# Thirty-three partly filled columns of a three-layer graph network, packed at lane offsets that are summed on the chip

## The chip, the cores and the metric

The kernel runs on one core of one Trainium2 chip. The metric is the device time of one execution in microseconds (us). Engines are named as the profile names them: PE (TensorE), DVE (VectorE), ACT (ScalarE), POOL (GpSimd) and SP (SyncE). SP computes nothing here; it issues plain DMAs. POOL issues the indirect DMAs (gathers and scatters).

## The reference

A graph of 6,250 nodes with 256 features and 100,000 edges (`src`, `dst`, sorted by `dst`) goes through two attention layers of one kind, a residual and a layer norm, and one attention layer of another kind, again with residual and layer norm.

```python
def _gatv2_layer(x, src, dst, n, Wl, Wr, att, b):          # H, C = 4, 64
    xl = (x @ Wl).reshape(n, H, C)
    xr = (x @ Wr).reshape(n, H, C)
    e = leaky_relu(xl[src] + xr[dst], 0.2)
    logits = einsum('ehc,hc->eh', e, att)
    ex = exp(logits - segment_max(logits, dst)[dst])
    alpha = ex / (segment_sum(ex, dst)[dst] + 1e-16)
    return segment_sum(xl[src] * alpha[:, :, None], dst).reshape(n, H * C) + b

# layers 1 and 2: every node is also its own neighbour; elu between them
x = layernorm(x + gatv2(elu(gatv2(x))))
# layer 3: 8 heads of 32; scores s1[src] + s2[dst], softmax per dst, weighted sum of Wh[src]
x = layernorm(x + gat(x))
```

The costly part is `xl[src]`: 100,000 rows of about 1 KB, fetched in each of three layers.

## The kernel before

**Plan.** `make_plan` sorts the nodes by how many edges they have, the most first, and cuts them into 49 blocks of 128 (a node per partition). For each node it makes a list of its sources, padded with the number of an empty row (NP, whose scores come out as minus infinity). Because nodes are sorted, a block needs few columns: `columns` computes, from the sizes of the problem alone (a Poisson distribution and 3.5 standard deviations), `cols[b]`, the columns of block b: 27 for block 0 (longer lists of that block are kept apart, the "few"), 25, 24, 23, ... down to 9, 803 in all. Block b, column j, is one gather: POOL fetches 128 rows, one per partition, by 128 indices (`gather_rows`, L1438).

**Packs before.** The last column of a block is often filled in its first partitions only. `columns` chooses ten such columns (blocks 3, 13, 17, 36; 26, 40, 47, 48; 31, 43) whose worst-case sizes, rounded up to eight, add up to at most 128, and joins them in three packs. SP copies the indices of a pack's columns to one column of `pick` (`pick_rows`, L1405), POOL gathers that column once (`gather_pack`, L1410), SP copies the rows from there to the place in each block's tile (`lay_rows`, L1418) and fills the other partitions of that column with the empty row (`lack_rows`, L1426). Places are known when the program is built.

**A layer.** `layer2` (layers 1 and 2) and the last part of `tile_by_degree` (layer 3) loop over the blocks. `gather(b)` puts block b's rows into two to four tiles `g` out of nine (`rowp`, bufs=9); a tile comes free when the block that held it has been summed. In layers 1 and 2 DVE computes the scores of a block (`attend`: L1797 or L1777, L1800, L1801), ACT the exponentials, DVE and ACT multiply rows by weights (L1633, L1629), PE adds them up (L1640), and PE makes the next layer's table rows, which SP stores (L1917, L1960). In layer 3 DVE does all of that but the exponentials. `fetch(b + 2)` is issued while block b is computed, so gathers run about two blocks ahead, as far as tiles allow.

**Order.** The order on each engine's queue is the order of the program's text (`manual_schedule`); each queue is worked in order and waits on semaphores. In layer 1 a block's node row (its source list and its features) is itself gathered by POOL, one gather a block (`start1`, L1887), called by `begins(b)`: three at the start, then `begins(b + 2)` in `fetch(b)`, and those that a pack's list needs. Between layers, the 37 first gathers of blocks 0 to 2 of the next layer (`begin`, lists `soon`) are taken from the part of the table that is complete early; the others wait until the whole table is written. `spots` are the sources' places in the sorted order, read in layer 1 out of the gathered rows' last element and used as lists in layers 2 and 3.

`counts` (L1270) holds each node's number of edges, and `fits` and `done` are flags: if the lists don't fit the planned shape, or the early part was too short, a general path (`tile_general_path`) does the work instead. `spare` (L1251 to 1257) is seven gathers of list pieces that nothing reads.

The lines that the steps of the prediction touch stand in the functions below.

Of the kernel before, what the change touches and what calls it, by code (L numbers as in the profile page):

```python
# [26 lines left out]
F32 = mybir.dt.float32  # L27
# [9 lines left out]
P = 128  # L37
# [10 lines left out]
def columns(E, N, NB):  # L48
# [30 lines left out]
    part = {}  # L79
    for b in range(len(EARLY), NB):  # L80
        c = cols[b] - 1
        n = max(8, -(-int(math.ceil(over[c] + 3.5 * sd[c] - P * b)) // 8) * 8)
        if n < P:
            part[b] = n
    packs, taken = [], set()
    for b in sorted(part):
        if b in taken or part[b] > P * 3 // 4:
            continue
        pack, at = [], 0
        for k in range(b, NB):  # L90
            if k in part and k not in taken and at + part[k] <= P:
                pack.append((k, at, part[k]))
                at += part[k]
        if len(pack) > 1:
            packs.append(pack)
            taken.update(k for k, _, _ in pack)
    return cols, low, high, held, packs
# [569 lines left out]
def kernel(  # L667
# [22 lines left out]
    cols, low, high, held, packs = columns(E, N, NB)  # L690
# [7 lines left out]
    node_i = plan.tile([P, NB], I32, name="node_i")  # L698
    fits = plan.tile([P, 1], I32, name="fits")
# [11 lines left out]
    with tc.manual_schedule():  # L711
        make_plan(
            tc, x, src, dst, ((wl1, wr1, att1), (wl2, wr2, att2)), (b1, b2), w3, a3,
            cols, low, high, held, packs, node_i, fits, ident, eps, nobody, att, wc, wh, fixed, xl1_d,
            near_d,
        )
        nc.vector.memset(done, 0)
# [4 lines left out]
    with tc.If(ok != 0):  # L722
        with tc.manual_schedule():
            tile_by_degree(
                tc, x, att1, b1, b2, w3, a3, out, [held] + cols[1:], packs, node_i, near_d, ident, eps, nobody,
                xl1_d, att, wc, wh, fixed, done,
            )
# [8 lines left out]
def make_plan(  # L736
    ctx, tc, x, src, dst, layers, biases, w3, a3, cols, low, high, held, packs, node_i, fits, ident, eps,
    nobody, att, wc, wh, fixed, xl1_d, near_d,
# [36 lines left out]
    SPARE = 7  # L775
# [218 lines left out]
    for pack in packs:  # L994
        for b, _, n in pack:
            nc.gpsimd.tensor_scalar(
                most[:, b : b + 1], part_of, float(n), float(cols[b] - 1), op0=OP.is_lt, op1=OP.add
            )
# [252 lines left out]
    spare = one.tile([P, SPARE, LONG], I32, name="spare")  # L1251
    left(1, nc.gpsimd)
    for k in range(SPARE):
        nc.gpsimd.indirect_dma_start(
            out=spare[:, k, :], out_offset=None, in_=listed,
            in_offset=bass.IndirectOffsetOnAxis(ap=begin_i[:, k : k + 1], axis=1),
        )
# [12 lines left out]
    counts = one.tile([P, NB], F32, name="counts")  # L1270
# [26 lines left out]
def tile_by_degree(  # L1297
    ctx, tc, x, att1, b1, b2, w3, a3, out, cols, packs, node_i, near_d, ident, eps, nobody,
    xl1_d, att, wc, wh, fixed, done,
# [52 lines left out]
    late = consts.tile([P, len(EARLY)], F32, name="late")  # L1352
# [41 lines left out]
    packed = {b: (q, r, n) for q, pack in enumerate(packs) for b, r, n in pack}  # L1394
    opens = {pack[0][0]: q for q, pack in enumerate(packs)}
    shuts = {pack[-1][0]: q for q, pack in enumerate(packs)}
    picks = [consts.tile([P, len(packs)], I32, name=f"pick{k}") for k in range(2)]
    for pick in picks:
        nc.gpsimd.memset(pick, NP)
    held_rows = {}  # L1400

    def pick_rows(q, pick, of):

        for b, r, n in packs[q]:
            nc.sync.dma_start(pick[r : r + n, q : q + 1], of[:n, b, cols[b] - 1 : cols[b]])  # L1405
# [710 lines left out]
```

## Time and profile before

| what | value |
|---|---|
| median of 3 runs | 3244.62 us (3239.51 to 3245.31) |
| profiled execution | 3236.04 us, span 3234.2 us |
| granted clock of PE, mean | 0.711 |
| DVE busy | 2714.0 us (84%) |
| POOL busy | 2414.4 us (75%) |
| PE busy | 1399.5 us (43%) |
| ACT busy | 1281.5 us (40%) |
| HBM | 354.60 MB read, 40.42 MB written |

How to read it: "busy" counts an engine's instructions; between two gathers POOL needs time that counts as idle with the releaser "issue". A line such as `L1438 POOL DMA_INDIRECT g<-xl_d,near_r x1549 | 1465.6, 946 | 472.6 <-issue 417.6` says: source line, engine, operation, what is written from what, how many; busy time, mean ns of one; idle time just before them and what ended it. The 40 digits are busy tenths of 40 equal slices of the span, 81 us each. Layer 1 begins with the first gather of rows at 102.9 us, layer 2's early gathers at 1158, layer 3's at 2155.

### The profile page before, as it was taken

The numbers are of one execution on the slowest core, as the hardware profiler recorded it, in microseconds if no ns is written. First come the engines' busy times: TensorE is split into PE (matmuls) and PEld (weight loads), VectorE is DVE, ScalarE is ACT, GpSimd is POOL, SyncE is SP. The second block draws the span as 40 slices with busy tenths as digits, with TensorE's granted clock in tenths as the row PEclk, the third lists the DMA queues.
The fourth block names the chain that finished last, engine by engine and source line by source line (L and its number), as shares of the span: only waits on it lengthen the run. The fifth ranks groups of instructions, "written<-read, shape, count | busy, mean of one in ns | idle before, by whom it ended". The sixth has DMA issues, their size and how long they took to land.

```text
span 3234.2 us, 25459 instructions
## 1 busy us (share of the span) xinstructions
PE 1399.5 (43%) x5423; PEld 1123.4 (35%) x5424; DVE 2714.0 (84%) x2609; ACT 1281.5 (40%) x5161; POOL 2414.4 (75%) x2587
## 2 busy tenths in 40 slices
PE   8356657666676854666556566760000000000000
PEld 6245545555565643545444455550000000000000
DVE  8599999898899979999989999984966766766777
ACT  4234444444445535777667777770000000000000
POOL 5677777777777777777777777777777777777776
PEclk9678888778888886787788778885555555555555
DMA  9444444444444454444444444444333333333333
GB/s 262 123 113 125 119 120 122 118 122 124 123 123 126 126 146 116 122 123 129 128 123 127 133 129 134 135 129 113 108 107 109 110 108 107 109 109 110 109 110 93
DMA packets 176463, 397.64 MB, mean 123 GB/s; under 512 B 50923, under 2 KB 93955, under 8 KB 176283
## 3 DMA queue, kind: packets, MB, share of 16 engines
q0 software_dynamic: 120608, 336.86, 38.7%
q1 hardware_dynamic: 53992, 57.08, 5.8%
q10 hardware_dynamic: 1700, 1.97, 0.2%
q8 instruction: 48, 0.79, 0.1%
q14 instruction: 115, 0.94, 0.1%
HBM read 354.60 MB, written 40.42 MB: 122 GB/s over the span
## 4 chain that ended last, share of the span: by engine, by line
POOL 25%; DVE 18%; issue 14%; DMA 5%; PE 3%; ACT 0%; DVEq 0%; POOLq 0%; ACTq 0%
POOL g L1438 24%; DVE z L1800 4%; DVE lg L1801 4%; DMA g<-xl_d,near_r 3%; DVE z L1797 3%; PE acc L1640 3%; DVE z L1777 2%; DVE g L1633 2%; DMA g<-whs_d,near_r 1%; DVE weighted L1662 1%; POOL out L2040 1%; DMA out<-y,node_i 1%; DVE stats L1684 0%; DVE acc_v L1674 0%; DVE at L1600 0%
## 5 line engine op out<-in xcount | busy, mean ns | idle before, releaser
L1438 POOL DMA_INDIRECT g<-xl_d,near_r x1549 | 1465.6, 946 | 472.6 <-issue 417.6
L1640 PE MATMUL acc<-g,ident 128*128 128x256 f32 x3408 | 966.5, 452 | 631.3 <-DVE g L1633 318.4
L1640 PEld LDWEIGHTS acc<-g,ident 128*128 128x128 f32 x3408 | 778.4, 232 | 820.4 <-DVE g L1633 336.3
L1438 POOL DMA_INDIRECT g<-whs_d,near_r x756 | 719.5, 952 | 230.3 <-issue 220.5
L1629 ACT ACTIVATE g<-g,by 128x64 f32<-128x64 f32 x3080 | 744.9, 336 | 28.4 <-DVE by L1596 28.4
L1801 DVE TENSOR_REDUCE lg<-z 128x28 f32<-128x1820 f32 (+4 forms) x234 | 497.3, 2125 | 8.1
L1800 DVE TENSOR_TENSOR z<-z,at 128x1820 f32<-128x1820 f32 (+4 forms) x234 | 496.6, 2122 | 4.7
L1797 DVE TENSOR_TENSOR z<-g,pr 128x1820 f32<-128x1820 f32 (+3 forms) x138 | 299.6, 2171 | 42.9 <-DMA g<-xl_d,near_r 33.7
L1604 ACT ACTIVATE wt<-lg 128x128 f32<-128x128 f32 (+17 forms) x49 | 14.0, 285 | 801.5 <-DVE lg L1603 801.5
L1674 DVE TENSOR_REDUCE acc_v<-weighted 128x256 f32<-128x3584 f32 (+10 forms) x47 | 319.0, 6787 | 1.6
L1633 DVE TENSOR_TENSOR g<-g,at 128x256 f32<-128x256 f32 (+8 forms) x185 | 273.5, 1496 | 3.3
L1587 ACT ACTIVATE at<-lg,top 128x19 f32<-128x19 f32 (+14 forms) x392 | 115.3, 294 | 378.2 <-DVE top L1579 359.5
L1777 DVE TENSOR_TENSOR z<-g,pr 128x2080 f32<-128x2080 f32 (+4 forms) x96 | 197.8, 2061 | 72.3 <-DMA g<-xl_d,near_r 33.3
L2010 DVE TENSOR_TENSOR lg<-g,s_r 128x56 f32<-128x56 f32 (+4 forms) x111 | 22.9, 214 | 255.5 <-DMA g<-whs_d,near_r 234.6
L1662 DVE TENSOR_TENSOR weighted<-g,wt 128x1792 f32<-128x1792 f32 (+4 forms) x111 | 227.0, 2056 | 0.3
L1563 ACT COPY xT<-pt 128x256 f32<-128x256 f32 x147 | 50.2, 374 | 403.4 <-PE pt L1558 403.4
L1568 PE MATMUL pm<-wcat,xT 128*128 128x260 f32 x392 | 94.2, 383 | 1.4 <-ACT xT L1563 1.4
L1568 PEld LDWEIGHTS pm<-wcat,xT 128*128 128x128 f32 x392 | 74.2, 190 | 13.3 <-ACT xT L1563 2.1
L1587 ACT ACTIVATION_READ_ACCUMULATOR at<-lg,top 128x1 f32 x392 | 73.2, 187 | 0.0
L1568 PE MATMUL pm<-wh_cat,xT 128*128 128x272 f32 x196 | 58.6, 422 | 22.6 <-ACT xT L1563 22.6
L2040 POOL DMA_INDIRECT out<-y,node_i x49 | 49.8, 1015 | 22.8 <-issue 14.1
L1688 ACT ACTIVATE sd<-mv,eps 128x1 f32<-128x1 f32 x98 | 29.0, 296 | 91.5 <-DVE mv L1686 91.3
(267 smaller groups left out, 1591.5 us busy)
## 6 DMA issues: line engine op xcount, KB each, us to landing
g<-xl_d,near_r POOLq DMA_INDIRECT x1549, 2.8
g<-whs_d,near_r POOLq DMA_INDIRECT x756, 2.8
whs_d<-row SPq DMA_DIRECT2D x49, 132.0 KB
xl_d<-row SPq DMA_DIRECT2D x49, 130.0 KB
xr_d<-row SPq DMA_DIRECT2D x49, 130.0 KB
two<-xl_d SPq DMA_DIRECT2D x49, 130.0 KB
two<-xr_d SPq DMA_DIRECT2D x49, 130.0 KB
near_d<-x_all SPq DMA_DIRECT2D x7, 896.0 KB
```

The costliest lines, as they stand in the source:

```text
L1438: nc.gpsimd.indirect_dma_start(out=g[:, j + own - s0, :width], out_offset=None, in_=table, in_offset=source(of, b, j),)
L1568: nc.tensor.matmul(pm, xT[:, c, :], w[:, c, :], start=c == 0, stop=c == 1)
L1587: nc.scalar.activation(wt[:, :, h], lg[:, :S, h], AF.Exp, bias=top[:, h : h + 1], accum_out=den[:, h : h + 1],)
L1629: nc.scalar.mul(g4[:, t, h, :], g4[:, t, h, :], by[:, s0 + t - a0, h : h + 1])
L1633: nc.vector.tensor_mul(g4[:, :m], g4[:, :m], wt[:, s0 : s0 + m, :].unsqueeze(3).to_broadcast([P, m, H, F // H]),)
L1640: nc.tensor.matmul(acc, ident, g4[:, t], start=False, stop=s0 + t == S - 1 and not more)
L1662: nc.vector.tensor_mul(prod[:, s0 - base : s1 - base, :].rearrange("p t (h d) -> p t h d", h=H), g[:, :n, :F].rearrange("p t (h d) -> p t ...
L1674: nc.vector.reduce_sum(part, prod[:, : s1 - base, :].rearrange("p s f -> p f s"), axis=AX.X)
L1777: nc.vector.tensor_max(z, rows[0][:, :n, :W2], xr[:, None, :].to_broadcast([P, n, W2]))
L1797: nc.vector.tensor_max(z, g[:, :n, :W2], xr[:, None, :].to_broadcast([P, n, W2]))
L1800: nc.vector.tensor_mul(z, z, at[:, None, :].to_broadcast([P, n, W2]))
L1801: nc.vector.reduce_sum(lg[:, s0:s1, :], z.rearrange("p t (h d) -> p t h d", h=H2), axis=AX.X)
```

## The change

The packs are made denser, and their places are no longer fixed when the program is built. `lanes_of` takes every column whose expected fill is under three quarters (0.75 x 128), the last ones of 28 blocks: 33 "items" (block, column), with a worst-case size `top` each and 781 - 11 = 770 columns left for gathers of their own (`base[b]`). `find_lanes` counts on the chip how many nodes really use each item's column (a comparison of `counts`, a sum over partitions on PE, a running sum on DVE): item i's rows begin at lane `at[i]`, the sum of those before it. Bounds `lo[i]` and `hi[i]` are known from the statistics; a value outside them sets the flag for the general path.

SP loads a lane into a register and writes the item's list, `top[i]` entries long, to that place in DRAM (`pick_lanes`); the next item's list overwrites the unused end. 14 columns of 128 entries are read back as `picks`, each one is one gather (`gather_packs`), the gathered rows are stored in DRAM (`keep_packs`, which in layer 1 also reads the places of the rows for the later layers), and each item's rows are read from its lane into its block's tile (`lay_rows`). The surplus rows of an item belong to others, so `shut_lanes` adds minus infinity to the scores of partitions that don't use the column. A pack is gathered a block before the first item that can reach it (`upon`); its list must be full by then, so `gather` in layer 1 calls `begins` for all blocks whose lists can fall into it. In layer 1 the packs' tiles are those of `two`, in layers 2 and 3 three of their own. The seven `spare` gathers and the per-partition limits `most` of packed columns are gone.

```diff
-    part = {}
...
-    return cols, low, high, held, packs
+    return cols, low, high, held, lanes_of(N, NB, mean, pmf, over, sd, cols, low, high)
...
-    for pack in packs:
-        for b, _, n in pack:
-            nc.gpsimd.tensor_scalar(
-                most[:, b : b + 1], part_of, float(n), float(cols[b] - 1), op0=OP.is_lt, op1=OP.add
-            )
...
-    for k in range(SPARE):
-        nc.gpsimd.indirect_dma_start(
-            out=spare[:, k, :], out_offset=None, in_=listed,
-            in_offset=bass.IndirectOffsetOnAxis(ap=begin_i[:, k : k + 1], axis=1),
-        )
...
+    upon = [max(1, b - 1) for b in need]
+    pick_d = dram.tile([K * P + P, 1], I32, name="pick_d")
+    wide = [W2 + 1, W2, A1]
+    pack_d = [dram.tile([K * P + P, w], F32, name=f"pack{k}_d") for k, w in enumerate(wide)]
+    nc.sync.dma_start(pick_d.rearrange("(k p) c -> p (k c)", p=P), nowhere)
...
+    def find_lanes(zp, ps):
+        for k, values in enumerate((lo, hi, [0] + top)):
...
+                    nc.vector.memset(bound[:, k, i:j], float(values[i]))
...
+        for b, own in items_of.items():
+            nc.vector.tensor_scalar(
+                has[:, own[0] : own[-1] + 1], numbers[:, base[b] : cols[b]], counts[:, b : b + 1],
+                None, op0=OP.is_lt,
+            )
+        nc.tensor.matmul(pn, ones, has, start=True, stop=True)
+        nc.vector.tensor_scalar(shut, has, -1.0, BIG, op0=OP.add, op1=OP.mult)
+        nc.vector.tensor_tensor_scan(at, ones[:, : len(items) + 1], n, 0.0, op0=OP.mult, op1=OP.add)
+        nc.vector.tensor_max(held_at, at, bound[:, 0])
+        nc.vector.tensor_tensor(held_at, held_at, bound[:, 1], op=OP.min)
+        nc.vector.tensor_copy(lane_i, held_at[:1, : len(items)])
...
+    def lane(i):
+        _, (v,) = nc.values_load_multi_w_load_instructions(
+            lane_i[:, i : i + 1], engines=[mybir.EngineType.SP], min_val=lo[i], max_val=hi[i],
+            skip_runtime_bounds_check_because="the lane was brought within these bounds",
+        )
+        nc.sync.nop()
+        return bass.ds(v, top[i])
+    def pick_lanes(lists):
+        while written[0] < len(items) and items[written[0]][0] < lists:
+            i = written[0]
+            b, c = items[i]
+            nc.sync.dma_start(pick_d[lane(i), :], sources[: top[i], b, c : c + 1])
+            for q in range(K):
+                if filled_by[q] == i:
+                    nc.sync.dma_start(picks[0][:, q : q + 1], pick_d[q * P : (q + 1) * P, :])
+            written[0] += 1
...
+    def gather_packs(b, pool, pick, table, width):
+        for q in packs_at.get(b, ()):
+            held_rows[q] = pool(q)
+            nc.gpsimd.indirect_dma_start(
+                out=held_rows[q][:, :width], out_offset=None, in_=table,
+                in_offset=bass.IndirectOffsetOnAxis(ap=pick[:, q : q + 1], axis=0),
+            )
+    def keep_packs(b, k):
+        for q in packs_at.get(b, ()):
+            nc.sync.dma_start(pack_d[k][q * P : (q + 1) * P, :], held_rows[q][:, : wide[k]])
+            if k == 0:
+                nc.sync.dma_start(picked[:, q : q + 1], pack_d[0][q * P : (q + 1) * P, W2 : W2 + 1])
+    def lay_rows(b, rows, cut, own, k):
+        for i in items_of.get(b, ()):
...
+            nc.sync.dma_start(g[: top[i], j - s0, : wide[k]], pack_d[k][lane(i), :])
+    def lack_rows(b, rows, cut, own, table, width):
...
+                nc.sync.dma_start(
+                    g[top[i] :, j - s0, :width],
+                    bass.AP(tensor=table.tensor, offset=table.offset + NP * width,
+                            ap=[[0, P - top[i]], [1, width]]),
+                )
+    def shut_lanes(b, lg, own, H):
+        if b in items_of:
+            s = lg[:, base[b] + own : cols[b] + own, :]
+            nc.vector.tensor_add(s, s, shut[:, i0 : i0 + n].unsqueeze(2).to_broadcast([P, n, H]))
...
             def gather(b):
-                if b in opens:
-                    gather_pack(b, packp, "pack", picks[i], table, width)
-                gather_rows(b, rows, cut, 1, table, of, width, first, cols[b])
...
+                if i == 0 and b:
+                    lists = max([b + 2] + [items[filled_by[q]][0] for q in range(K) if upon[q] <= b]) + 1
+                    for k in range(min(NB, lists)):
+                        begins(k)
+                    pick_lanes(lists)
+                gather_rows(b, rows, cut, 1, table, of, width, first, base[b])
+                gather_packs(b, pack_tile, picks[i], table, width)
+                lack_rows(b, rows, cut, 1, table, width)
+                if b == 1:
+                    waiting.append(lambda: (keep_packs(b, i), lay_rows(b, rows, cut, 1, i)))
+                else:
+                    lay_rows(b, rows, cut, 1, i)
+                    waiting.append(lambda: keep_packs(b, i))
...
+                shut_lanes(b, lg, 1, H2)
...
             if i == 0:
                 find_few(work, pst)
+                find_lanes(zp, pst)
+                pick_lanes(3)
             gather(0)
...
+    nc.scalar.copy(picks[1], picked)
...
         def gather(b):
...
+            while waiting:
+                waiting.pop(0)()
+            gather_rows(b, rows, cut, 0, wh_d[:, :], spots, A1, first, base[b])
+            gather_packs(b, pack_tile, picks[1], wh_d[:, :], A1)
+            lack_rows(b, rows, cut, 0, wh_d[:, :], A1)
...
```

(`shut_lanes` is called in both `attend` functions, before the softmax; the last `gather` is that of layer 3.) Packs are gathered at blocks 1 (three), 3, 5, 7, 8, 15, 19, 20, 25, 34, 44 and 46. The lists that they need end with the columns of blocks 8, 16 and 20 for the three of block 1, then 25, 30, 35, 39, 42, 44, 46, 47 and 48.

## The prediction

> **What bounds the kernel now.** I read the page first: shares by engine, the 40 slices, the costliest groups.
>
> ```profile
> PE 1399.5 (43%) x5423; PEld 1123.4 (35%) x5424; DVE 2714.0 (84%) x2609; ACT 1281.5 (40%) x5161; POOL 2414.4 (75%) x2587
> ...
> DVE  8599999898899979999989999984966766766777
> ...
> POOL 5677777777777777777777777777777777777776
> ...
> L1438 POOL DMA_INDIRECT g<-xl_d,near_r x1549 | 1465.6, 946 | 472.6 <-issue 417.6
> ...
> L1438 POOL DMA_INDIRECT g<-whs_d,near_r x756 | 719.5, 952 | 230.3 <-issue 220.5
> ```
>
> DVE has the larger share, but POOL never varies. A gather is 946 ns busy and then 0.30 us in which POOL waits for nothing ("issue"), so one gather costs 1.25 us, and 75% busy is POOL full. Then the waits, POOL's and DVE's:
>
> ```profile
> POOL g L1438 <- issue: 658.0, 2160, 0.3
> ...
> DVE lg L2010 <- DMA g<-whs_d,near_r: 234.6, 40, 9.0
> ...
> DVE z L1797 <- DMA g<-xl_d,near_r: 33.7, 27, 3.4
> DVE z L1777 <- DMA g<-xl_d,near_r: 33.3, 19, 6.0
> ...
> POOL g L1438 <- PE acc L1640: 27.1, 86, 1.1
> ```
>
> From 98 us on POOL practically waits for nobody, and DVE waits for gathers: much in the third layer, little in the first two. Busy time by layer (about 102 to 1158, to 2155, to the end):
>
> ```profile
> 102.00:1158.00 1056.00, 685.36 (x2689) 559.06 (x2690) 960.95 (x859) 457.70 (x1877) 798.76 (x845) 0.81 0.45 121
> 1158.00:2155.00 997.00, 612.41 (x2232) 482.99 (x2231) 922.97 (x781) 699.21 (x2879) 753.76 (x797) 0.80 0.47 129
> 2155.00:3234.00 1079.00, 23.66 (x88) 16.96 (x86) 752.14 (x814) 83.92 (x263) 808.66 (x850) 0.51 0.39 108
> ```
>
> (Columns: PE, PEld, DVE, ACT, POOL, clock, DMA share, GB/s.) DVE is busy 91% and 93% of layers 1 and 2 and 70% of layer 3. So a gather less is worth 1.25 us in layer 3, and in layers 1 and 2 only where DVE still waits. Last, the boundary of layers 1 and 2: the last store of SP into the table (it landed 2.47 us after its issue), and POOL's first gather that needs the whole table.
>
> ```profile
> 1194.19 2.47 DMA xl_d<-row
> ```
>
> ```profile
> 1203.34 0.95 POOL L1438 DMA_INDIRECT g<-xl_d,soon  x1 [0.30 <-issue]
> 1204.59 0.95 POOL L1438 DMA_INDIRECT g<-xl_d,near_r  x1 [0.30 <-issue]
> ```
>
> The table is whole at 1196.7; POOL comes to it 7.9 us later, after its 37 early gathers. At the next boundary the last row goes out at 2185.84 (landed about 2188.3) and POOL comes at 2201.65.
>
> **The change, part by part.** *Gathers.* Row gathers fall from 1549 + 756 to 1503 + 733 (69 less), pack gathers rise from 9 to 42: 36 less, 12 a layer, 15.0 us of POOL a layer. The seven spare gathers (74.6 to 84.4 us) go too; I cost that at nothing, because POOL's next work waits 3.15 us for DVE's list of moves after them. The ten TENSOR_SCALARs at 14.5 us stand before a 16.5 us wait: nothing.
>
> *Node rows moved forward (layer 1).* A pack gather needs its list full, so `begins` now loads the node rows (L1887, 1.25 us each) of far later blocks first: 18 of them right before block 1's gathers instead of 4; by block 8 there are 40 in all instead of 14, by block 25 there are 48 instead of 32. None is added, but DVE starves early. Counting POOL instructions to the end of block 25: 531 before, 544 after (16 more node rows, 13 less rows, 10 more packs), so POOL is there 16.3 us later, at 783.8 for 767.5, and with DVE's 9.8 us behind it block 25's scores are done at 793.5 instead of 777.3. From block 26 to 48 DVE took 401.2 us, 382.3 busy. With POOL ahead the 18.9 us between go: wherever DVE lags 11 us or more in this trace (blocks 5 to 7, 42 to 46) its idle time is 0.0 to 0.6 us a block. Added: 14 of the new `shut_lanes` additions there, 0.20 us each by the nearest row (L1491, 128x44), 2.8. So DVE ends layer 1 at +16.2 - 18.9 + 2.8 = +0.1; I take +2 for waits on ACT that stay. Ends: 0, and +20 if no idle time is regained. Layer 1 keeps nothing of its 15 us.
>
> *The list chain on SP (new wait).* Each of the 33 columns is a register load, a nop and a list write to DRAM, and the writes overlap, so each waits for the one before; 14 of them and three reads stand before POOL's three pack gathers of block 1. Nearest rows: SP's TENSOR_LOAD took 0.76 us (L721), a list copy 0.62 us to issue (L1405), a store 2.47 us to land, the slowest landing of a write to DRAM 7.5 (near_d<-moved). A link is then 2.5 us at least, 9.0 at most (7.5 + 0.76 + 0.17 + 0.62 in a row); I take 2.6, since the load runs in the shadow of the write and xl_d<-row is the nearest in size. Node row 3 lands near 142, ten links and a read follow: 142 + 11 x 2.6 = 171. POOL's packs come at 160.5 + 23 x 1.25 = 189.3. Hidden by 18 us; it costs from 4.3 us a link on, 11 us of stall for each us more, 52 at most; an added wait can't gain, so the other end is 0. Queued behind the waiting pack gather are all later gathers. `find_lanes` before it holds DVE about 13 us (85 memsets of 0.06, 28 compares and a dozen others of 0.15 to 0.2) while it would start block 0, which is then still being gathered (POOL till 136.8): nothing. It also gives the register loads.
>
> *Lanes back to tiles.* Packs are stored (42 stores), read back (99 lanes instead of 30 copies), 54 fills instead of 30. SP is in order, and behind its waits stand the table stores, which nobody needs before a layer's end. A pack lands 2.8 us after its gather, is in DRAM 2.5 us later, and a lane in the tile after a load (1.0) and about 2.5 more: 9 to 10 us, against a following block of 14 to 28 us of gathers. In layer 1 block 1 has no such cover: its lanes come near 206, so its scores near 214 instead of 185.4. That lateness is not added, since block 7 and block 25 are set by POOL's count above. Cost 0, and no gain is possible; if the cover went, up to 10 us at each of the 12 blocks that gather packs.
>
> A rule speaks against this part. The rows: DMA engines are 0.39 to 0.47 busy in all layers, SP's queue 5.8%. The Trainium skill (DMA: Bandwidth & Descriptors, section Bandwidth) calls transfers under 64 KB descriptor-dominated and wants 1 MiB; its 64 KB take 0.95 us. By that estimate 111 more pieces are 105 us of DMA time, which as a serial cost would turn the forecast into a loss of 73 us; by the rows they lie beside the gathers and cost nothing.
>
> *Layer 2.* POOL is done with layer 1 at 1142.8 (15 us sooner) and would come to its 27th early gather at 1175.3, but that needs block 48's first tile, free near 1187 (PE's sums at 1182.5 plus half of 4.6, plus 2): 1187 + 11 x 1.25 = 1200.7. Gain at the boundary 4 us, not 15. Blocks 1 to 10 run at DVE's pace, 11 to 37 at POOL's, which by block 37 has 6 gathers less: -4 - 7.5 = -11.5. After that DVE sets the pace again and gains nothing more, but POOL has 6 less still: it comes to layer 3's whole table at 2201.65 - 4 - 15 = 2182.7. The table is whole at 2188.3 - 11.5 + 2 = 2178.8. Layer 3 starts 19 us sooner.
>
> *Layer 3.* DVE idles 4 to 8 us a block, so 12 gathers are 15 us. At the end blocks 47 and 48 are down to 8 and 6 gathers; DVE needs 10.6 us a block, and about 2 us are lost.
>
> **Sum:** -4 - 15 - 15 + 2 = -32 us. The profiled execution took 3236.0 us (span 3234.2), so 3204; it lies 8.6 under the median of 3244.6, for which I say 3213.
>
> **The rivals.** (A) DVE holds layers 1 and 2: its idle time there isn't regained. Layer 1 then ends 20 late, the table is whole at 1216.7, layer 2 starts 12 late, gains nothing and pays 28 x 0.2 us; layer 3's table comes at 2206, 4 late, and its 13 us are all that's left: -9, 3236. For it: DVE's 91 and 93%. Against: the idle-free blocks with lag. (B) The whole count is gained, 45 us, 3200, if both boundaries follow POOL. Against it: the tile that the early gathers need, and 9s in DVE's row at the end of layer 1. (C) Slower: POOL stalls at the three pack gathers of block 1 in layer 1, for list links of 9.0 us: 142 + 99 = 241 instead of 189.3, 52 us, net +20, 3265. It turns the sign from 7.2 us a link on. For it: 7.5 us landings exist. Against: those were 171 KB, a list is 512 B. The change could also not take at all, if a lane left its bounds and the flag sent the work to the general path; the inputs' degrees give 1,670 rows, 13.05 packs of 14, so I leave that out.
>
> **How the numbers follow.** Forecast 0.50, A 0.22, B 0.10, C 0.15, anything else 0.03. About 0.2% (6.5 us) is what a measurement can tell from no change. A straddles that edge a little: faster 0.77, same 0.08, slower 0.15. The range runs from under B (3197) to over A (3241), and leaves C and the rest out.
>
> **What would show it.** Right: 1503 + 733 row gathers at 946 ns; POOL's first wait-free stretch unbroken near 189 us; block 1's first layer scores near 214; POOL idle for several us near 1176 to 1187, before the early gathers of block 2; layer 3's first whole-table gather near 2183. Wrong: POOL idle before a pack gather released by an SP copy (C), or DVE's idle time of blocks 26 to 48 in place though POOL is ahead (A).

## The result and the profile after

The changed kernel took 3282.62 us (median of 4 runs, 3275.27 to 3284.55) beside 3244.1 us of the kernel before: a ratio of 1.0117, with a 95% interval of 1.0099 to 1.0136. The change makes the kernel slower by 38 us; the forecast was 3213 us, and its range ended at 3241. The profiled execution took 3275.3 us (span 3273.5), 39.3 us of span more than the profiled execution before (3234.2). All profile comparisons below are against that span.

In five of the seven later comparisons, on four chips that I call "the slower chip", the kernel before takes 3807 to 3845 us instead of 3234 to 3245 and engines stand without a visible releaser, so every ratio is to the kernel before in the same comparison, and no kernel time of the one kind of chip is set against one of the other.

The page of the changed kernel first (the lines that answer to those of before: busy shares, the slices of DVE, POOL and DMA, the two groups of row gathers).

```profile
PE 1402.7 (43%) x5425; PEld 1125.8 (34%) x5426; DVE 2735.3 (84%) x2817; ACT 1280.7 (39%) x5162; POOL 2369.1 (72%) x2533
...
DVE  8529889989999997999999999994976776667676
...
POOL 4547777777777767777777777777777777777775
...
DMA  9756754564545545444445445554444344443443
...
L1536 POOL DMA_INDIRECT g<-xl_d,near_r x1503 | 1421.5, 946 | 471.6 <-issue 404.4
...
L1536 POOL DMA_INDIRECT g<-whs_d,near_r x733 | 695.8, 949 | 223.3 <-issue 207.2
```

The gathers are what the change promises: 1503 + 733 at an unchanged 946 ns, POOL busy 45 us less. But POOL's row now has a 4 in the third slice (from about 164 us), DVE's a 2 there, and the DMA engines, 9 in the first slice, stay at 7, 5 and 6. The waits (engine, line, what released it; us in total, times, longest) say what stands there:

```profile
POOL g L1536 <- issue: 633.4, 2064, 3.5
POOL two L1493 <- DMA pick<-pick_d: 43.7, 4, 23.7
POOL g L1536 <- PE acc L1738: 35.9, 63, 17.0
...
DVE lg L2123 <- DMA g<-whs_d,near_r: 214.8, 43, 7.9
DVE z L1881 <- DMA g<-xl_d,near_r: 65.0, 14, 22.4
DVE z L1901 <- DMA g<-pack_d: 38.6, 1, 38.6
```

The second line is POOL before a pack gather, waiting for a list that SP reads back from DRAM; the last is DVE, once, for the lanes of a block. The timeline of POOL shows where (start, duration, and in brackets the idle time before):

```profile
198.81 0.95 POOL L1536 DMA_INDIRECT g<-xl_d,near_r  x1 [0.30 <-issue]
200.06 0.95 POOL L1493 DMA_INDIRECT two<-xl_d,pick  x1 [0.30 <-issue]
224.67 0.94 POOL L1493 DMA_INDIRECT two<-xl_d,pick  x1 [23.67 <-DMA pick<-pick_d]
236.92 0.94 POOL L1493 DMA_INDIRECT two<-xl_d,pick  x1 [11.30 <-DMA pick<-pick_d]
```

These are the three pack gathers of block 1 in layer 1: 35 us of standing. SP's own timeline and its queue's waits show why the lists are late:

```profile
162.69 19.73 SPq L1479 DMA_DIRECT2D pick_d<-near_r  x3
192.15 0.34 SPq L1482 DMA_DIRECT2D pick<-pick_d  x1
```

```profile
SPq L1479 <- DMA pick_d<-near_r: 107.9, 19, 9.4
SPq L1482 <- DMA pick_d<-near_r: 98.7, 13, 10.3
```

Three list writes stretch over 19.73 us, of which the last one's issue is 0.35: (19.73 - 0.35) / 2 = 9.7 us a link. Every line "pick_d<-near_r" in the waits is a list write or a list read that waits for the list write before it, up to 10.3 us. The prediction had 2.6.

The busy time by layer (columns as before: PE, PEld, DVE, ACT, POOL, clock, DMA share, GB/s; the borders are again the first early gathers of the next layer):

```profile
112.00:1216.00 1104.00, 683.95 (x2682) 557.74 (x2683) 970.47 (x1008) 455.03 (x1870) 786.21 (x831) 0.80 0.56 119
1216.00:2201.00 985.00, 608.53 (x2224) 480.04 (x2223) 924.30 (x807) 695.52 (x2864) 742.71 (x785) 0.80 0.50 134
2201.00:3273.00 1072.00, 29.10 (x102) 21.66 (x102) 763.05 (x848) 89.31 (x286) 796.18 (x837) 0.51 0.42 112
```

Layer 1 is 48 us longer, layers 2 and 3 are shorter, and the clock is the same within 0.01. In layer 1 the DMA engines are busy 0.56 instead of 0.45 although they move less (119 GB/s for 121). Last, the boundary of layers 1 and 2, where the prediction put the first of its gains:

```profile
1198.58 0.95 POOL L1536 DMA_INDIRECT g<-xl_d,near_r  x1 [0.30 <-issue]
1216.49 0.95 POOL L1536 DMA_INDIRECT g<-xl_d,soon  x1 [16.96 <-PE acc L1738]
...
1261.86 0.95 POOL L1536 DMA_INDIRECT g<-xl_d,soon  x1 [0.30 <-issue]
1263.12 0.95 POOL L1536 DMA_INDIRECT g<-xl_d,near_r  x1 [0.30 <-issue]
```

POOL, ahead of DVE by then, waits 17 us before its first early gather, not before the 27th, and has all 37 still to do after it (46.6 us). What it waits for is read further below, with the lanes 64 B apart.

Five points of the timeline split the 39.3 us: the first row gather of layer 1, the first gather that needs the whole table of layer 2, the same of layer 3, the last output's issue, and the end.

| us | before | after | difference of the stretch |
|---|---|---|---|
| first row gather | 102.9 | 112.9 | start +10.0 |
| layer 2's whole table | 1204.6 | 1263.1 | layer 1 +48.5 |
| layer 3's whole table | 2201.7 | 2247.9 | layer 2 -12.3 |
| last output's issue | 3228.2 | 3261.1 | layer 3 -13.3 |
| end of span | 3234.2 | 3273.5 | tail +6.4 |

### The profile page after: what moved, and what is told of

Its sections match the earlier page's. It is cut to its first block, busy times and chain, and to the rows that moved or that the text cites. A ratio compares the mean times of both kernels' runs of the same rounds, so it can differ in the third digit from the quotient of the medians.

```text
span 3273.5 us, 26519 instructions
## 1 busy us (share of the span) xinstructions
PE 1402.7 (43%) x5425; PEld 1125.8 (34%) x5426; DVE 2735.3 (84%) x2817; ACT 1280.7 (39%) x5162; POOL 2369.1 (72%) x2533
## 4 chain that ended last, share of the span: by engine, by line
POOL 21%; DVE 18%; issue 12%; DMA 7%; PE 3%; ACT 2%; DVEq 0%; POOLq 0%; ACTq 0%
POOL g L1536 20%; DVE z L1904 4%; DVE lg L1905 4%; DMA g<-whs_d,near_r 3%; PE acc L1738 3%; DMA g<-xl_d,near_r 3%; DVE z L1901 2%; DVE z L1881 2%; DVE g L1731 2%; ACT g L1727 1%; DMA out<-y,node_i 1%; POOL out L2154 1%; DVE weighted L1760 1%; DVE acc_v L1772 0%; DVE stats L1782 0%
## 5 line engine op out<-in xcount | busy, mean ns | idle before, releaser
L1536 POOL DMA_INDIRECT g<-xl_d,near_r x1503 | 1421.5, 946 | 471.6 <-issue 404.4
L1536 POOL DMA_INDIRECT g<-whs_d,near_r x733 | 695.8, 949 | 223.3 <-issue 207.2
```

What stands on the lines that cost most here:

```text
L1536: nc.gpsimd.indirect_dma_start(out=g[:, j + own - s0, :width], out_offset=None, in_=table, in_offset=source(of, b, j),)
```

## The experiments

My theory after this reading: the list chain on SP is the loss, through POOL's wait for it. Rivals: the node rows moved forward, or DVE, which would have no room in layer 1. Open inside the theory: why a write of 512 B lands after 9 us, whether POOL's wait or SP's lateness counts, and what the slow start is.

**The chain taken away, the node rows alone, and the lanes spread out (slower chip).** The kernel without the chain leaves out 33 list writes (with their register loads) and 14 list reads; its packs gather fixed rows, so 33 columns get other rows than they should, but nothing else changes in number or size.

```
+    nc.gpsimd.iota(picks[0], pattern=[[3, K]], base=0, channel_multiplier=48)
 def pick_lanes(lists):
-            nc.sync.dma_start(pick_d[lane(i), :], sources[: top[i], b, c : c + 1])
-            for q in range(K):
-                if filled_by[q] == i:
-                    nc.sync.dma_start(picks[0][:, q : q + 1], pick_d[q * P : (q + 1) * P, :])
```

> The changed kernel without its list chain in layer 1: the 33 list writes into pick_d and the 14 reads into picks are left out, and the packs gather 14 x 128 fixed rows spread over the table instead (so the rows of the 33 columns are not the right ones; every gather, store, lane copy and addition stays in number and size). Theory 1 (the list chain on SP is the loss: links of 4 to 10 us instead of the 2.6 that the prediction took, so POOL stands before the three pack gathers of block 1 until 200, 225 and 237 us): those gathers come 23 row gathers after block 1's first, near 190 to 200 us, block 1's first scores near 195 to 215 instead of 256, and the time falls by about 55 to 70 us, to 3210 to 3230. Rival (the node rows moved forward, or DVE in layers 1 and 2, are the loss): block 1 is as late as before and the time stays above 3265.

The node rows alone, in the kernel before:

```
 def gather(b):
+    if i == 0 and b:
+        lists = max([b + 2] + [t for u, t in zip(upon, until) if u <= b]) + 1
+        for k in range(min(NB, lists)):
+            begins(k)
```

> The kernel before with one part of the change alone: its node rows are loaded in the order of the changed kernel (18 of them before block 1's row gathers, 40 by block 8, 48 by block 25), and nothing else. Theory 1: 14 more node rows of 1.25 us delay block 1 by 17 to 20 us, and the delay is gone again by the end of layer 1, where DVE's 18.9 us of idle time in blocks 26 to 48 are used up: 3240 to 3252. Rival (front-loading is the loss): the 20 us stay, or more where the loads crowd the DMA engines: 3262 to 3285.

The lanes spread out, in the changed kernel:

```
-    pick_d = dram.tile([K * P + P, 1], I32, name="pick_d")
+    pick_d = dram.tile([K * P + P, 128], I32, name="pick_d")
-            nc.sync.dma_start(pick_d[lane(i), :], sources[: top[i], b, c : c + 1])
+            nc.sync.dma_start(pick_d[lane(i), 0:1], sources[: top[i], b, c : c + 1])
```

(and the fill and the reads likewise).

> The changed kernel with the lanes of the list in DRAM 512 B apart instead of 4 B (only the first number of a row of 128 is used); the same 33 list writes with the same elements and the same waits. If the slow links come from 4-byte writes to neighbouring addresses, which wait for each other: a list of 128 lands after 2.5 to 3.5 us instead of 8 to 10, the pack gathers of block 1 come at 190 to 205 us, and the time falls to 3215 to 3235. If the number of small writes sets the landing, whatever their addresses: links stay at 6 to 10 us and the time at 3275 to 3290.

The expected times were for a chip like the first and can't be held against these: the kernel before took 3827.35 us here. As ratios: without the chain 1.001 (0.9976 to 1.0043), node rows alone 0.9978 (0.9951 to 1.0005), spread lanes 1.0099 (1.0066 to 1.0132). Front-loading is no loss. The links can be read here too: with lanes 512 B apart, full lists of 128 numbers in block 1's chain follow each other after 1.4 to 1.5 us. The chain's first link alone took 7.0 us, and there SP's own small instructions took 0.7 us each. Two were run again:

> The changed kernel with the lanes of the list in DRAM 512 B apart instead of 4 B, run again beside the kernel before. Address theory (4-byte writes to neighbouring addresses wait for each other): a list of 128 numbers lands within 1.4 to 3 us instead of 7 to 10, the three pack gathers of block 1 come at 185 to 205 us instead of 200, 225 and 237, block 1's first scores near 205 to 220 instead of 256, and the time falls by 45 to 70 us against the changed kernel, to 0.988 to 0.997 of the kernel before. If the number of small writes sets the landing: 1.01 of the kernel before, as the changed kernel.

> The changed kernel without its list chain in layer 1 (33 list writes and 14 list reads left out, the packs gather fixed rows), run again beside the kernel before. Theory 1 (the chain is the loss): 0.985 to 0.997 of the kernel before, and no more than 10 us from the kernel with spread lanes, since with links of 1.4 us the chain should hide behind POOL's row gathers. Rival (node rows forward, or DVE): above 1.006.

Spread lanes 1.0074 (1.005 to 1.0099), without the chain 0.9896 (0.9851 to 0.994). The first missed what was expected: its links were 1.4 us, yet its three pack gathers came at 217 to 227 us, because DVE had the lane numbers only at 194 us: PE stood for 71.7 us, without a visible releaser, before the matmul that counts them (6.3 us on the first chip). So a control, and the fill:

> The changed kernel once more, unedited, as the control for the runs beside it: on the first chip it took 1.0117 of the kernel before (1.0099 to 1.0136). If the chip of this call is like the first, the same again. On a chip where every kernel is some 18% longer, because engines wait for their instructions, other waits cover part of the chain's, and a ratio between 1.005 and 1.02 is to be expected; the links of the list chain stay at 7 to 10 us for 128 numbers, since they depend on the writes alone.

```
-    nowhere = consts.tile([P, K + 1], I32, name="nowhere")
+    nowhere = twop.tile([P, 2, W2], F32, name="two").bitcast(I32)[: K + 1, 0, :P]
-    nc.sync.dma_start(pick_d.rearrange("(k p) c -> p (k c)", p=P), nowhere)
+    nc.sync.dma_start(pick_d.rearrange("(k p) c -> k (p c)", p=P), nowhere)
```

> The changed kernel with its first fill of pick_d written as 15 rows of 512 B instead of 1,920 single numbers of 4 B. If that fill delays the first node row (it landed 11.5 us after its issue): it lands after about 3 us, and the first row gather of layer 1 comes 8 to 10 us sooner after the node row's issue than in the changed kernel. The list chain still waits for the lanes and still sets block 1, so of the 10 us only 0 to 10 arrive at the end: 0.997 to 1.000 of the changed kernel. If the three pack_d fills delay it: no change.

The changed kernel 1.0359 (1.0324 to 1.0394), more than expected; the fill 1.0309 (1.029 to 1.0329). The control's full lists follow each other after 6.1 to 9.7 us in block 1's chain, so the links are long on this kind of chip too when the lanes lie side by side. On the slower chip the change costs 3.6%; with the lanes spread it cost 0.7 and 1.0%, though in other comparisons, so some 2.7% hang on the addresses. The two profiles don't tell the fill's part: in the control SP issued the fill 2.9 us after the first node row, and the row gathers began 5.3 us after it, 5.7 with rows of 512 B.

**Packs in layers 2 and 3 alone, and lanes 64 B apart (a chip like the first).** Layer 1 gathers its 33 columns itself, and the lists are written from the places kept for the later layers:

```
-                gather_rows(b, rows, cut, 1, table, of, width, first, base[b])
-                gather_packs(b, pack_tile, picks[i], table, width)
+                gather_rows(b, rows, cut, 1, table, of, width, first, base[b] if i else cols[b])
+                if i:
+                    gather_packs(b, pack_tile, picks[i], table, width)
...
 nc.scalar.copy(spots[:, b, s - 1 : s1 - 1], g[:, s - s0 : s1 - s0, W2])
+pick_lanes(b + 1)
```

> The changed kernel with its packs in layers 2 and 3 alone: layer 1 gathers the 33 columns with row gathers of its own (27 + ... = 803 gathers instead of 784 after and 796 before), loads its node rows in the order of the kernel before, and writes the 33 lists (lanes 512 B apart) from the places that it keeps for the later layers, a block's lists after its scores; POOL waits for no list in layer 1. Theory 1 (layers 2 and 3 gain what the change set out to gain, and all of the loss lies in layer 1's wait for the lists): layer 1 takes 0 to 9 us more than before (7 gathers of 1.25 us), layers 2 and 3 together 20 to 30 us less on a chip like the first, 30 to 45 on one where all engines wait for instructions: 0.987 to 0.996 of the kernel before, and never slower than the kernel with spread lanes and packs in layer 1. If the loss lies in the lanes' way back to the tiles (99 copies, which layers 2 and 3 keep): 1.000 to 1.010.

> The changed kernel with the lanes of the list 64 B apart in DRAM (one number of a row of 16 is used), between the 4 B of the changed kernel and the 512 B of the spread one. If writes hold each other up only within the same few bytes (64 B or less): a list of 128 lands in 1.4 to 2 us as with 512 B, and the time is that of the spread kernel, 1.005 to 1.012 of the kernel before on a chip where that one took 1.007 to 1.010. If it is a stretch of 512 B that they share (8 lists' numbers in each): links of 3 to 7 us, and a time between 1.010 and 1.036.

The kernel before took 3233.8 us here. Packs in layers 2 and 3 alone: 3229.98 us, 0.9987 (0.9977 to 0.9996), a gain, but less than expected, and, against what was expected, slower than the kernel that has spread lanes and packs in layer 1 as well. That one, with lanes 64 B apart: 3220.43 us, 0.9961 (0.9947 to 0.9975). A change of one address stride turns a loss of 1.2% into a gain of 0.4%, and this version beats both kernels. Its pack gathers of block 1, its list writes and SP's longest wait that has to do with them:

```profile
190.28 0.95 POOL L1536 DMA_INDIRECT g<-xl_d,near_r  x1 [0.30 <-issue]
191.53 0.95 POOL L1493 DMA_INDIRECT two<-xl_d,pick  x1 [0.30 <-issue]
192.78 0.95 POOL L1493 DMA_INDIRECT two<-xl_d,pick  x1 [0.30 <-issue]
194.03 0.95 POOL L1493 DMA_INDIRECT two<-xl_d,pick  x1 [0.30 <-issue]
```

```profile
152.68 7.18 SPq L1479 DMA_DIRECT2D pick_d<-near_r  x4
```

```profile
SPq L1479 <- DMA near_r<-near_d,node_i: 79.3, 11, 17.5
```

Four list writes in 7.18 us are 2.3 us a link ((7.18 - 0.33) / 3; single links 1.4 to 2.7), SP's longest wait in the chain is now for a node row (17.5 us) and for its own list writes 2.8 us at most, and POOL passes from row gathers to pack gathers without a gap. The number of small writes is the same as before, so their number alone doesn't make them slow: writes of 4 B to neighbouring addresses hold each other up, and at 64 B no longer.

They hold up others too. The DMA queues between 112 and 205 us (packets, MB, share of the 16 engines' time; q0 is POOL's, that is the gathers), of the kernel before, of the changed kernel and with lanes 64 B apart:

```profile
q0 software_dynamic: 3564, 10.03, 39.9%
```

```profile
q0 software_dynamic: 3452, 9.96, 83.1%
```

```profile
q0 software_dynamic: 3557, 10.22, 42.0%
```

The same gathers' packets take twice the time while the neighbouring writes are under way.

**POOL's wait against SP's lateness.** The whole slow chain stays on SP, but the lists go to a tile that nobody uses and the packs gather fixed rows, so POOL doesn't wait:

```
+    nc.gpsimd.iota(picks[0], pattern=[[3, K]], base=0, channel_multiplier=48)
+    heard = consts.tile([P, K], I32, name="heard")
-                    nc.sync.dma_start(picks[0][:, q : q + 1], pick_d[q * P : (q + 1) * P, :])
+                    nc.sync.dma_start(heard[:, q : q + 1], pick_d[q * P : (q + 1) * P, :])
```

This comparison, with repeats of the others, is on the slower chip:

> The changed kernel without its list chain in layer 1 (33 list writes and 14 list reads left out, the packs gather fixed rows). Theory 1 (the chain is the loss): the packs come at 190 to 195 us, as with lanes 64 B apart, and the time is within 6 us of that kernel, 0.993 to 0.998 of the kernel before. If the short chain of 1.4 to 2.7 us a link still costs something: 0.985 to 0.993. If something other than the chain is the loss: above 1.005.

> The kernel before with the changed kernel's order of node rows alone (18 before block 1's row gathers, 40 by block 8, 48 by block 25). Theory 1: block 1 is 17 to 20 us late, the end of layer 1 0 to 5 us, and the time within 0.999 to 1.002 of the kernel before. If front-loading is a loss of its own: block 48 of layer 1 ends 15 to 20 us late, 1.004 to 1.007.

> The changed kernel with its first fill of pick_d written as 15 rows of 512 B instead of 1,920 numbers of 4 B; the list chain is as slow as in the changed kernel. If the fill delays the first node row: it lands within 4 us of its issue instead of 11.5, and the first row gather comes at 103 to 106 us instead of 112.9. POOL's row gathers end 8 to 10 us sooner at block 0; the chain, which starts with the lanes, is no sooner, so at the end 0 to 5 us remain: 1.010 to 1.0125 of the kernel before. If the start adds up with the rest: 1.0085.

> The changed kernel with its whole slow list chain on SP, but with packs that gather fixed rows in layer 1 and so don't wait for the lists (the list reads go to a tile that nobody uses). If POOL's stand before the pack gathers (35 us) is what counts: the packs come near 200 us without a wait, and the time falls by 30 to 40 us, to 0.999 to 1.002 of the kernel before. If SP's queue counts as much (block 1's lanes are copied behind the whole chain, at 245 us): block 1's scores stay near 250 us, POOL waits for tiles instead, and the time stays above 1.007.

Without the chain 0.9923 (0.9894 to 0.9952), node rows alone 0.9973 (0.9947 to 0.9998), fill 1.0346 (1.0295 to 1.0398), without POOL's wait 0.9992 (0.9959 to 1.0026). So again front-loading costs nothing, POOL's wait is as much as the whole 3.6% of the earlier control, and SP's lateness is 0.7% beyond it (0.9992 against 0.9923). These profiles tell the fill's part at the start: without the chain but with the dense fill ahead of it, the row gathers begin 12.5 us after the first node row's issue, with the fill as rows 5.4. The next comparison was on a chip like the first:

> The changed kernel with its whole slow list chain on SP, but with packs that gather fixed rows in layer 1 and so don't wait for the lists. On the slower chip this gave back 3.7 of the 3.6% that the change lost. On a chip like the first, where POOL stands 35 us before the pack gathers of block 1: if that stand is the loss, 0.999 to 1.003 of the kernel before; if SP's late lane copies of block 1 (DVE waits for them until 250 us) hold the later gathers as long, above 1.007.

> The changed kernel without its list chain in layer 1 (list writes and reads left out, the packs gather fixed rows). On a chip like the first: 0.993 to 0.998 of the kernel before, as the kernel with lanes 64 B apart (0.9961), whose packs never waited; on the slower chip 0.990 to 1.001, as before.

Without POOL's wait 3243.1 us, 1.0029 (1.0016 to 1.0041); without the chain 3226.26 us, 0.9975 (0.9965 to 0.9985). The profiles say what remains in the first of them: POOL passes into the packs at 195.13 us without a gap, but SP is still behind, and DVE stands for the lanes of block 1:

```profile
DVE z L1903 <- DMA g<-pack_d: 33.6, 1, 33.6
```

The last pair, on the slower chip again:

> The kernel before with the changed kernel's order of node rows alone (18 before block 1's row gathers, 40 by block 8, 48 by block 25). On a chip like the first: block 1 is 17 to 20 us late, the end of layer 1 0 to 5 us, 0.999 to 1.002 of the kernel before; on the slower chip it was 0.9973 to 0.9978. If front-loading is a loss of its own: 1.004 to 1.007.

> The changed kernel with its first fill of pick_d written as 15 rows of 512 B instead of 1,920 numbers of 4 B; the list chain is as slow as in the changed kernel. On a chip like the first: first row gather at 103 to 106 us instead of 112.9. If the start adds up with the rest, 1.0085 of the kernel before; if the chain covers it, 1.010 to 1.0125. On the slower chip it was 1.031 to 1.035 beside 1.036 of the changed kernel.

Node rows alone 0.9972 (0.9952 to 0.9992), fill 1.034 (1.0288 to 1.0393). The fill as rows shows no gain in the whole time that could be measured there; on a chip like the first it was not measured alone.

The stretches of the profiled executions on the first kind of chip, as differences to the kernel before in us:

| | start | layer 1 | layer 2 | layer 3 | tail | sum | medians of all runs |
|---|---|---|---|---|---|---|---|
| changed kernel | +10.0 | +48.5 | -12.3 | -13.3 | +6.4 | +39.3 | +38.5 |
| slow chain kept, POOL does not wait | +5.9 | +12.5 | -12.5 | -13.6 | +6.3 | -1.4 | +9.2 |
| no chain | +5.4 | +1.3 | -11.8 | -12.7 | +6.4 | -11.4 | -7.6 |
| lanes 64 B apart | +2.1 | +0.7 | -12.3 | -12.9 | +6.3 | -16.1 | -13.4 |
| packs in layers 2 and 3 alone | +2.9 | +8.9 | -12.6 | -12.0 | +8.3 | -4.5 | -3.8 |

The last column is each kernel's median less the median of the kernel before in the same comparison. The second row's profiled execution, 3234.6 us, is the shortest of its six; the median is 8.5 us longer. Of the changed kernel's 58.5 us up to layer 2's whole table, by these single executions, POOL's wait is 58.5 - 18.4 = 40.1, SP's lateness 18.4 - 6.7 = 11.7, and 6.7 have nothing to do with the chain. By the medians it is 38.5 - 9.2 = 29.3 for POOL's wait and 9.2 + 7.6 = 16.8 for SP's lateness. So the chain costs 46 to 52 us, POOL's wait is the larger part, and the split is known to some 11 us only. The packs in layer 1 are worth having once the lists are quick: they cost 0.7 us there, and own gathers cost 8.9, which are the 7 more gathers of 1.25 us (8.75).

## Why the prediction was wrong, point by point

**The step that failed: the list chain on SP.** The prediction said "A link is then 2.5 us at least, 9.0 at most [...]; I take 2.6, since the load runs in the shadow of the write and xl_d<-row is the nearest in size", and "Hidden by 18 us". The load does run in the shadow of the write. The landing was wrong: 9.7 us a link in the stretch that counts, 6.7 to 10.3 for a full list of 128 in block 1's chain, so the bound of 9.0 was itself too low. That bound rested on a misread row: 7.5 us, "the slowest landing", is the median of the writes near_d<-moved in the kernel before, and the slowest took 9.1, which would have made the bound 10.6:

```profile
DMA to landing us min/median/max: 5.1/7.5/9.1
```

"Nearest in size" was the wrong likeness. A row of xl_d is 1,040 B in one piece per partition; a list of 128 numbers is 128 pieces of 4 B side by side. No row before the change writes pieces as small as that to DRAM next to each other, and that should have kept the price near the upper end. With 64 B between the lanes the links are 1.4 to 2.7 us, and with them the times up to block 25 that were built on 2.6 come within 3 us: packs at 191.5 us (predicted 189.3), block 1's first scores at 216.8 (214), POOL at the end of block 25 at 784.2 (783.8), block 25's scores at 795.3 (793.5).

Rival C was the case that came: "POOL idle before a pack gather released by an SP copy", with 52 us of stall for links of 9.0. On the trace POOL stands 35 us there. Its mechanism was right, and its chance of 0.15 was too low. That the chain as a whole costs 40.1 + 11.7 = 51.8 us up to layer 2 in the profiles is luck for C's 52: 11.7 of it are SP's lateness, which C didn't have. C's sum was net +20 us; measured +38, mostly because the gains that it is netted with were smaller, as told below.

**"That lateness is not added."** With quick lists this holds. With slow ones it doesn't: with POOL's wait gone and the chain kept, DVE stands 33.6 us for block 1's lanes, and 11.7 us of that reach layer 2 (16.8 of the whole time by the medians).

**What the prediction left out: the start.** It costed the spare gathers at nothing, which holds: the first node row is issued at 97.1 to 100.4 us in the five profiles on the first kind of chip that are without them, at 99.0 before. But it never priced the first fill of `pick_d`, 1,920 numbers side by side, that SP issues just ahead of that node row. The row landed 11.5 us after its issue instead of 2.9. With lanes 64 B apart the row gathers begin 6.1 us after the node row's issue, without the chain but with the dense fill 11.2, before 3.9. What this is worth at the end on a chip like the first was not measured.

**Node rows moved forward: right in the main.** Front-loading is no loss, and DVE does regain its idle time, against rival A, but not quite all of it. With lanes 64 B apart block 25's scores are 18.0 us late (795.3 for 777.3). SP issues the last row for layer 2's table at 1201.7 us instead of 1194.2: 7.5 us late, where the prediction took 2. In the kernel before, the node rows alone were tried on the slower chip only, three times, with ratios of 0.9972 to 0.9978.

**The boundary of layers 1 and 2, and layer 2.** "Gain at the boundary 4 us, not 15" became a loss of 2.7 (1207.3 for 1204.6, lanes 64 B apart). The prediction expected POOL to wait there for a tile, before the 27th early gather, with 11 gathers after it. The wait lies before the first, 16.6 us long, with 37 after it, and it is for a row of the table. The early gathers read blocks 0 to 44 of it (`AHEAD`, 45 x 128 rows). The kernel before, then lanes 64 B apart, each with SP's store of block 44's row and POOL's first early gather:

```profile
1153.62 0.33 SPq L1917 DMA_DIRECT2D xl_d<-row  x1
1157.97 0.94 POOL L1438 DMA_INDIRECT g<-xl_d,soon  x1 [0.43 <-PE acc L1640]
```

```profile
1143.25 0.95 POOL L1536 DMA_INDIRECT g<-xl_d,near_r  x1 [0.30 <-issue]
1158.01 0.33 SPq L2022 DMA_DIRECT2D xl_d<-row  x1
1160.80 0.94 POOL L1536 DMA_INDIRECT g<-xl_d,soon  x1 [16.60 <-DVE row L1989]
```

The view names a DVE instruction as the releaser, but by the trace's semaphores the store landed at 1160.03 us and the wait of POOL's sequencer ended at 1160.05. In all four kernels with packs in layer 1 (this one, the changed one, no chain, POOL not waiting) the gather starts 2.8 to 3.5 us after that store's issue. Before, this row was ready just when POOL came (0.43 us). POOL now arrives 13.3 us earlier and starts these gathers 2.8 us later, because block 44's row, at DVE's pace, is stored 4.4 us later. Whether the 27th gather would have waited for a tile can't be seen, since POOL comes to it later than predicted. Layer 2 from there to layer 3's table was expected at 2182.7 - 1200.7 = 982.0 and took 984.8: -12.3 us for -15.

**Layer 3: right.** -15 for 12 gathers, and about 2 lost at the end, gave -13; measured -12.7 to -13.6 in the kernels with all packs.

**The tail: not foreseen.** After the last output's issue the kernel before takes 6.0 us to its end, every kernel with the new packs 12.3 or more, on both kinds of chip. It is in no row of the groups; it lies in two closing instructions of POOL's sequencer, a semaphore increment and a drain, 1.72 + 6.28 us for 0.46 + 1.14.

So the sum of the prediction, -32, is -16.1 with lanes 64 B apart: missing are 6.7 us up to layer 2's table (+2.7 for -4; 2.1 of them from the start), 2.7 in layer 2, 0.1 in layer 3 and 6.3 in the tail, 15.8 in all. The other 55 us of span, from -16.1 to +39.3 (52 by the medians), are the dense addresses.

The rule that was weighed, that small transfers are dominated by their descriptors (the Trainium skill, DMA: Bandwidth & Descriptors, section Bandwidth), was set aside since the pieces "lie beside the gathers". That was right for the lane copies and stores of layers 2 and 3, which took back at most the 2.7 us that layer 2 misses. (The 105 us that were worked out by the rule counted 111 pieces; the 24 more fills named just before would have made them 135.) The same page's section Specifications has a rule that the prediction should have weighed as well: below 512 B a transfer does not reach line rate, and the DMA engine reads, modifies and writes. The runs agree with it half way: dense writes of 4 B took 9.7 us a link, but writes of 4 B that lie 64 B apart, as far below 512 B, took 1.4 to 2.7. The size alone doesn't make them slow. Whether the DMA engine reads and modifies around them, no run here shows.

## What to carry to other kernels

Price a transfer by the row nearest in the shape of its pieces and in their addresses, not in its bytes; where no row has pieces so small and so close, take the upper end and look at who waits behind it. Where single numbers are written to DRAM, leave 64 B from one to the next: here it cost only space (between 4 and 64 B nothing was tried). When you take a landing time from a profile as a bound, take the longest, not the median. And when an engine is given less work, ask at each boundary for which tile or which row of a table it will stand once it is early, and count what it still has to do after that.

## What the runs showed of the hardware that was not expected

- A write of 128 numbers of 4 B to neighbouring DRAM addresses was followed by the next link after 6.7 to 10.3 us in block 1's chain, the two lists of 8 numbers in layer 1 after 1.4 and 2.5; with 64 B or 512 B from number to number, one of 128 in block 1's chain after 1.4 to 2.7, but for the first link on the slower chip (7.0 and 7.7, SP's own instructions). That the addresses make it is shown; what in the memory makes it is not.
- While such writes are under way the packets of the gathers take twice as long on the DMA engines (83.1% of the 16 engines' time instead of 42.0% for the same 10 MB).
- The kernel's closing drain was 1.1 us before, 6.3 with the new packs and 7.8 with packs in layers 2 and 3 alone; the first two were the same to 0.01 us on both kinds of chip. What sets it stays open; nothing here was tried on it.
